# Reordering quarter products around a split S1 T1, in a relational graph layer on one core

## Chip, cores and metric

The kernel runs on one core of one Trainium2 chip. The metric is the device time of one execution in microseconds (us), as the median of several runs. Beside it there is one profiled execution, from which all durations of single instructions come.

## What is computed

A graph layer over N = 1250 nodes with D = 1024 features, R = 8 edge types and 20000 edges, all in fp32:

```python
h = maximum(layernorm(x), 0)
u = h @ root + bias
for r in range(8):                       # mean over the edges of type r into a node
    u = u + (segment_sum(h[src] * mask_r, dst) / maximum(cnt_r, 1)) @ weight[r]
z = concatenate([u, h]) @ w_gate + b_gate
out = x + tanh(u) * z + h * (1 - z)
```

## The kernel before

**Matrices and pairs.** The kernel multiplies first and sums over edges later. It forms h times each of the eight edge-type matrices (numbers 0 to 7), h times `root` (8) and h times the lower half of `w_gate` (9), stores these rows to HBM, and gathers them per edge. The last stage multiplies the finished u by the upper half of `w_gate` (10). The 1250 nodes are ten blocks of 128 rows, taken as five *pairs* (i = 0 to 4). So the outer loop is over matrices s = 0 to 9, the inner one over pairs, each a call of `step(s, i)`.

**One pair's product.** `product` (L388) multiplies two row blocks by a 1024x1024 matrix with seven products of half size instead of eight (the Winograd form of Strassen's method). Each has 128 rows, 512 of the inner dimension and 512 columns, and is four calls in `add` (L401), each of which is two TensorE instructions of 512 columns. Names: P1 = A11 B11, P2 = A12 B21, P3 = S4 B22, P4 = A22 T4, P5 = S1 T1, P6 = S2 T2, P7 = S3 T3. S are sums of blocks of h, T sums of blocks of the matrix (`make_t1` to `make_t4`, on VectorE). P1, P6, P7 and P4 build up in one PSUM bank `b`, and after each ScalarE copies the running sum out (L445, L468, L427, L493) before the next may be added. P5 goes to a bank `c`, is copied (L453), and P3 is added to it.

**Quarter products.** Pairs 0 and 1, and pairs 2 and 3, share work once more: the two P2 products of such a pair of pairs are done together by seven quarter products (class `Second`, object `e`). From matrix 4 on (`thirds(s)`) the same is done for P3 (class `Third`, `q`) and P1 (class `First`). A quarter product is `Second.add` at L218: four instructions of 256 columns. The fifth pair (i = 4) has no partner and is called the lone pair here; it does P2 and P3 itself.

**PSUM.** There are eight banks: a ring of four named `ps` (`bank()`), two named `ps_b` (`lead()`), and one each of `ps_q` and `ps_n`. A bank is written again only after its readers are done.

**Order of the work.** Every engine works through its own list in program order, and this order is written by hand. `done()` (L407) counts the steps of a product and calls `between(j)`. That hook puts other engines' work beside TensorE's: sums on VectorE, weight loads on the ScalarE and SyncE queues, and the edge work (a gather by GpSimd into one of four buffers at L1268, then multiply and add into a node's row on VectorE at L1273), spread evenly over the steps, seven to a product. `filled(name)` puts the quarter products behind the named product, by the dictionary `fill` in `step` (L623 to L657).

In pairs 0 and 2, P5 comes first, into `ps_n` (`hold`, L283). `First.late` (L350) then gives P1: six calls, and a copy at L353. In pair 0, `e.second` follows (with its add at L249), then P6, then P7 at once. In pairs 1 and 3, `then` (`Third.last` and `last_to`, L300 to L317) runs three quarter products between P6 and P7, and VectorE adds them at L313, L314 and L315. Pair 3 begins with `e.fourth`, which adds to a bank that ScalarE has just copied at L235; `q.first` (L290) comes behind it, and `e.second` between P7 and P4.

`First.early` (L339), the first four quarter products of a coming pair's P1, runs ahead of P4 in pairs 1 and 4. Behind it VectorE makes the sums of L278 to L281 for `First.late`. The sums of L272 to L275 serve `First.early`, and in pairs 0 and 2 `Third.first`.

**Row tiles.** Results collect in row tiles, of which there are four, each stored to HBM by SyncE (`put`, L551). The two tiles of pair 4 are those of pair 2. One of these is complete only in pair 3, and is stored there, after the add at L249.

Of the kernel before, what the change touches and what calls it, by code (L numbers as in the profile page):

```python
# [9 lines left out]
F32 = mybir.dt.float32  # L10
# [9 lines left out]
def tile_rgcn_highway(  # L20
# [35 lines left out]
    P = 128  # L56
# [4 lines left out]
    KQ = KC // 2  # L61
# [59 lines left out]
    def bank():  # L121
        return psum.tile([P, 512], F32, name="ps", bufs=4)
# [135 lines left out]
    class Third:  # L258
# [29 lines left out]
            Second.add(self, c[:, :H], self.a12, self.b21)  # L288

        def first(self):  # L290
            self.b = psum.tile([P, 512], F32, name="ps_q", bufs=1)[:, :H]
            self.c = bank()[:, :H]
            self.p = rows.tile([P, Q], F32, name="part", bufs=2)
            Second.add(self, self.b, self.a11, self.b11, True)
            nc.scalar.copy(self.p[:, :H], self.b)
            Second.add(self, self.c, self.s1, self.t1, True)
            Second.add(self, self.b, self.s2, self.t2)
            nc.scalar.copy(self.p[:, H:], self.b)
# [87 lines left out]
                                                                     aop[:, b])  # L386

    def product(aop, w, to, between=lambda j: None, last=None, pieces=1, whole=True,  # L388
                fill=None, second=None, third=None, inner=None, first=None, early=None):

        c11, c12 = to[0][:, :Q], to[0][:, Q:]
        c21, c22 = to[1][:, :Q], to[1][:, Q:]
        step = [0]

        def add(b, i, fresh=False, at=slice(0, Q)):  # L401
            for k in range(KQ):
                nc.tensor.matmul(b[:, at], aop[:, i, k, :], w.of[i][:, k, at],  # L403
                                 start=(fresh and k == 0), stop=(k == KQ - 1),
                                 skip_group_check=True)

        def done():  # L407
            between(step[0])
            step[0] += 1

        def filled(name):
            if fill and name in fill and fill[name]():
                done()

        def p3():
            add(c, S4)
            if third:
                third(c)
            else:
                nc.vector.tensor_add(c12, c12, c)  # L420
            done()
            filled("third")

        def p7():
            d = rows.tile([P, Q], F32, name="part", bufs=2)
            add(b, S3)
            nc.scalar.copy(d, b)  # L427
            nc.vector.tensor_add(c22, c22, d)  # L428
            done()
            filled("seventh")  # L430
            return d

        def p2():
            a = bank()
            add(a, A12, True)
            nc.vector.tensor_add(c11, c11, a)
            done()

        def p1():
            if first is None:  # L440
                b = lead()
                add(b, A11, True)
            else:
                b = first.late() if inner.holds else first.to1
            nc.scalar.copy(c11, b)  # L445
            done()
            filled("first")
            return b

        def p5():  # L450
            c = inner.hold() if inner and inner.holds else bank()
            add(c, S1, True)
            nc.scalar.copy(c22, c)  # L453
            done()
            filled("fifth")
            return c

        if first and inner.holds:
            c = p5()
            b = p1()  # L460
        else:
            b = p1()
            if second:
                second()
                p2()
            c = p5()
        add(b, S2)
        nc.scalar.copy(c12, b)  # L468
        done()
        filled("sixth")  # L470
        if whole and not third:
            p3()
            d = p7()
            if not second:
                p2()
        else:
            if inner and not inner.holds:
                inner.then(c)
                done()
                filled("third")  # L480
            d = p7()
            if third:
                last(d, 0)
            if not inner:
                p3()
        if early:
            early()
        if pieces == 1:
            add(b, A22)
            if last:  # L490
                last(b, 0)
            else:
                nc.scalar.copy(c21, b)  # L493
        else:
            for j in reversed(range(pieces)):
                at = slice(j * Q // pieces, (j + 1) * Q // pieces)
                b = bank()
                add(b, A22, True, at)
                last(b[:, at], at.start, d[:, at])
        done()  # L500
        filled("fourth")
# [27 lines left out]
    def step(s, i, between=lambda j: None, second=None):  # L529
# [80 lines left out]
        if two:  # L610
            e, to = waiting[i - i % 2]
            if thirds(s):
                if i % 2 == 0:
                    waiting_third[i] = Third(fac[s], i, room)
                q = waiting_third[i - i % 2]
                q.holds = i % 2 == 0

                def then(c):
                    q.last(c)
                    q.last_to(to[:, Q:], t[0][:, Q:], c)  # L620

                q.then = then
            if i == 0:  # L623
                fill = dict(sixth=lambda: (e.second(), e.second_to_first(to)))
                if q:
                    fill = dict(first=fill["sixth"], seventh=lambda: (q.second(q.c0), True))
            elif i == 1:
                fill = dict(first=lambda: (e.first(), q and q.first(), 0)[-1],
                            fifth=lambda: (e.sixth(), True),
                            sixth=lambda: (e.seventh(), e.to_first(to), 0)[-1])  # L630
                if q:
                    fill.update(third=lambda: (e.fourth(), e.to_second(t[0]),
                                               put(i - 1, 0, to), 0)[-1],
                                seventh=lambda: (e.fourth_to_second(t[0]), 0)[-1])
                else:
                    fill.update(seventh=lambda: (e.fourth(), e.to_second(t[0]),
                                                 put(i - 1, 0, to), 0)[-1],
                                third=lambda: (e.fourth_to_second(t[0]), 0)[-1])
            elif i == 2 and q:
                fill = dict(first=lambda: e.first(),  # L640
                            sixth=lambda: (q.second(q.c0), True),
                            seventh=lambda: e.sixth(),
                            fourth=lambda: (e.seventh(), e.to_first(to), True))
            elif i == 2:
                fill = dict(sixth=lambda: e.first(),
                            seventh=lambda: e.sixth(),
                            third=lambda: (e.seventh(), e.to_first(to), 0)[-1],
                            fourth=lambda: (e.fourth(), True))
            elif q:
                fill = dict(first=lambda: (e.fourth(), e.to_second(t[0]),  # L650
                                           e.fourth_to_second(t[0]), q.first(), 0)[-1],
                            seventh=lambda: (e.second(), True),
                            fourth=lambda: (e.second_to_first(to), put(i - 1, 0, to), 0)[-1])
            else:
                fill = dict(first=lambda: (e.to_second(t[0]), e.fourth_to_second(t[0]), 0)[-1],
                            sixth=lambda: (e.second(), True),
                            seventh=lambda: (e.second_to_first(to), put(i - 1, 0, to), 0)[-1])  # L657
        product(h_op[i], fac[s], t, between=beside, whole=not two, fill=fill, second=second,
                inner=q, first=waiting_first.get((s, i - i % 2)) if two else None,
                early=early if coming else None)  # L660
        for part in range(2):
            if part or not two or i % 2:
                put(i, part, t[part])
# [80 lines left out]
    with ExitStack() as early:  # L744
# [226 lines left out]
        def slots(ix):  # L971
# [78 lines left out]
            def place(j):  # L1050
                cs, o = chunks(j), now.pop(j)
                m, c0 = len(cs), cs[0]
                c1 = c0 + m
                p = psum.tile([P, 512], F32, name="ps_q", bufs=1)
                for i in range(m):
                    nc.tensor.matmul(p[:, i * 2 * NHI:(i + 1) * 2 * NHI], o["to_lo"][:, i, :],
                                     o["s_b"][:, i].rearrange("p a b -> p (a b)"),
# [184 lines left out]
    with ExitStack() as edges_part:  # L1242
# [358 lines left out]
        for i in range(NP):  # L1601
# [49 lines left out]
                    scatter_piece(c0, t[1])  # L1651

            if i < NP - 1:
                product(h_op[i % 2], fac[NM - 1], t, between=beside_u,
                        last=lambda *of: finish(1, *of))
                outs.append((2 * i + 1, t[1]))
            else:
                product(h_op[i % 2], fac[NM - 1], t, between=beside_last, last=finish_last,
                        pieces=2, second=lambda: None,
                        third=lambda c: finish(0, c, Q, rows.tile([P, Q], F32, name="part",  # L1660
                                                                  bufs=2)))
# [22 lines left out]
```

## Time and profile before

| what | value |
|---|---|
| median of 3 runs (lowest to highest) | 1363.49 us (1363.39 to 1367.92) |
| the profiled execution: time | 1361.2 us |
| the profiled execution: span, first to last instruction | 1359.4 us |
| VectorE, ScalarE, GpSimd busy | 73%, 28%, 44% of the span |
| granted TensorE clock, mean | 0.997 |
| bytes moved by DMA | 271.18 MB, 199 GB/s in the mean |
| one matrix of 4 to 9, start to start | 117 to 122 us |

The span is the profile's own measure; the execution's time is 1.8 us more. In the rows of a profile, PE is TensorE's matmuls, PEld its weight loads, DVE VectorE, ACT ScalarE, POOL GpSimd, SP SyncE. `L403` is line 403 of the kernel. `ps_b<-w,h_op` means that `ps_b` is written from `w` and `h_op`. `128x512` are partitions and elements of one instruction. Line 403 is every full product, line 218 every quarter product, and the bank's name tells which.

### The profile page before, as it was taken

Reading aid. Unit: us, or ns where it says so; the run is one execution under the profiler, and the core shown is the slowest. Engines: PE = TensorE matmul, PEld = TensorE weight load, DVE = VectorE, ACT = ScalarE, POOL = GpSimd, SP = SyncE. Lnnn points to the kernel's source line nnn. Section 1 sums busy time; section 2 is a strip of 40 time slices with the busy share of each in tenths; the row PEclk is TensorE's granted clock in tenths of the full one; section 3 lists DMA queues with packets and bytes.
Section 4 is the critical chain, followed back from the end, with each engine's and each line's share of the span. In section 5 each row is a group of like instructions: output and inputs, shape, how many; then the busy total and the mean of one; then the engine's idle time right before and its main releaser. Section 6 shows DMA issues by size and latency. Waiting matters only on the chain. (4 is left out here: it accounts for less than half of the span.)

```text
span 1359.4 us, 13672 instructions
## 1 busy us (share of the span) xinstructions
PE 1336.1 (98%) x4098; PEld 712.2 (52%) x4098; DVE 995.2 (73%) x2049; ACT 384.1 (28%) x852; POOL 592.6 (44%) x510
## 2 busy tenths in 40 slices
PE   9999999999999999999999999999999999999997
PEld 5444455455445545655664555565465456644443
DVE  7855967876785835526877887987778789777875
ACT  3335566465741112211121211122122111221210
POOL 0001655654652466001454554555455546534731
PEclk9999999999999999999999999999999999999999
DMA  9744675754764251144647778788778958889961
GB/s 317 271 177 150 103 131 143 210 84 110 175 166 111 54 153 34 47 155 151 206 132 293 241 237 320 281 262 307 245 248 294 337 180 239 265 286 286 350 169 58
DMA packets 106911, 271.18 MB, mean 199 GB/s; under 512 B 22692, under 2 KB 24946, under 8 KB 106704
## 3 DMA queue, kind: packets, MB, share of 16 engines
q1 hardware_dynamic: 46640, 120.01, 29.2%
q0 software_dynamic: 44064, 118.28, 27.5%
q10 hardware_dynamic: 16128, 31.98, 7.4%
q8 instruction: 32, 0.52, 0.2%
q14 instruction: 47, 0.39, 0.1%
HBM read 212.71 MB, written 75.66 MB: 212 GB/s over the span
## 5 line engine op out<-in xcount | busy, mean ns | idle before, releaser
L403 PE MATMUL ps_b<-w,h_op 128*128 128x512 f32 x1560 | 702.1, 595 | 5.0 <-ACT row L468 4.1
L403 PEld LDWEIGHTS ps_b<-w,h_op 128*128 128x128 f32 x1560 | 291.6, 190 | 334.5 <-issue 316.9
L1268 POOL DMA_INDIRECT got<-y,idx x193 | 261.6, 1355 | 335.8 <-DVE u L1273 206.0
L403 PE MATMUL ps<-w,h_op 128*128 128x512 f32 (+1 forms) x760 | 340.3, 591 | 3.0 <-ACT row L453 3.0
L1273 DVE SCALAR_TENSOR_TENSOR u<-got,w_of,u 128x1024 f32<-128x1024 f32 (+1 forms) x193 | 246.9, 1282 | 54.1 <-DMA got<-y,idx 47.3
L1084 POOL DMA_INDIRECT table<-row_col,at_i x157 | 175.5, 1118 | 160.0 <-DVE at_i L1080 76.9
L403 PEld LDWEIGHTS ps<-w,h_op 128*128 128x128 f32 x760 | 143.8, 191 | 167.7 <-issue 161.2
L427 ACT COPY part<-ps_b 128x512 f32<-128x512 f32 x55 | 32.2, 585 | 218.2 <-PE ps_b L403 218.2
L428 DVE TENSOR_TENSOR row<-row,part 128x512 f32<-128x512 f32 x54 | 37.2, 689 | 70.2 <-ACT part L427 70.2
L493 ACT COPY row<-ps_b 128x512 f32<-128x512 f32 x49 | 28.6, 584 | 185.8 <-PE ps_b L403 185.8
L468 ACT COPY row<-ps_b 128x512 f32<-128x512 f32 x54 | 31.6, 585 | 146.0 <-PE ps_b L403 145.9
L218 PE MATMUL ps<-w,h_op 128*128 128x256 f32 x264 | 69.0, 384 | 2.8 <-ACT w L235 2.8
L218 PE MATMUL ps<-w,w 128*128 128x256 f32 x288 | 71.3, 380 | 0.0
L218 PEld LDWEIGHTS ps<-w,w 128*128 128x128 f32 x288 | 54.4, 190 | 20.9 <-issue 14.8
L218 PEld LDWEIGHTS ps<-w,h_op 128*128 128x128 f32 x264 | 49.1, 190 | 26.6 <-issue 16.1
L453 ACT COPY row<-ps 128x512 f32<-128x512 f32 x42 | 24.6, 585 | 120.1 <-PE ps L403 104.4
L1070 DVE SCALAR_TENSOR_TENSOR junk<-k_bc,key_col,before 128x128 f32<-128x128 int32 x157 | 55.0, 350 | 4.2
L1010 DVE TENSOR_TENSOR seen<-seen,ps_n 128x100 f32<-128x100 f32 x157 | 40.2, 256 | 24.3 <-PE ps_n L1005 20.1
L445 ACT COPY row<-ps_b 128x512 f32<-128x512 f32 x54 | 31.7, 587 | 89.8 <-PE ps_b L403 83.7
L173 DVE TENSOR_TENSOR w<-w,w 128x2048 f32<-128x2048 f32 (+1 forms) x12 | 25.4, 2115 | 41.4 <-PE ps L403 41.2
L218 PE MATMUL ps<-inner,inner 128*128 128x256 f32 x192 | 49.4, 380 | 1.2 <-DVE inner L273 1.2
L420 DVE TENSOR_TENSOR row<-row,ps 128x512 f32<-128x512 f32 x29 | 19.8, 684 | 41.9 <-PE ps L403 30.7
(236 smaller groups left out, 1460.2 us busy)
## 6 DMA issues: line engine op xcount, KB each, us to landing
y<-row SPq DMA_DIRECT2D x72, 512.0 KB
w<-in_L_gnn_weight_dram ACTq DMA_DIRECT2D x21, 1024.0 KB
w<-in_L_gnn_weight_dram SPq DMA_DIRECT2D x10, 1024.0 KB
k_bc<-keys_dram SPq DMA_DIRECT2D x39, 256.0 KB
l_bc<-los_dram SPq DMA_DIRECT2D x39, 256.0 KB
w<-in_L_gnn_w_gate_dram ACTq DMA_DIRECT2D x6, 1024.0 KB
h_dram<-h_op SPq DMA_DIRECT2D x9, 512.0 KB
u<-in_L_gnn_bias_dram SPq DMA_DIRECT2D x9, 512.0 KB
```

The costliest lines, as they stand in the source:

```text
L218: nc.tensor.matmul(p, a[:, k, :], b[:, k, :], start=(fresh and k == 0), stop=(k == 1), skip_group_check=True)
L403: nc.tensor.matmul(b[:, at], aop[:, i, k, :], w.of[i][:, k, at], start=(fresh and k == 0), stop=(k == KQ - 1), skip_group_check=True)
L427: nc.scalar.copy(d, b)
L428: nc.vector.tensor_add(c22, c22, d)
L445: nc.scalar.copy(c11, b)
L468: nc.scalar.copy(c12, b)
L493: nc.scalar.copy(c21, b)
L1010: nc.vector.tensor_add(seen[j][:, i, :], was, p[:, i, :])
L1070: nc.vector.scalar_tensor_tensor(junk, o["k_bc"][:, i, :], key_col[:, c:c + 1], before, op0=OP.is_equal, op1=OP.mult, accum_out=rank[:, c: ...
L1084: ins = nc.gpsimd.indirect_dma_start(out=table[:, :], out_offset=bass.IndirectOffsetOnAxis(ap=at_i[:n, i:i + 1], axis=0), in_=row_col[:n, ...
L1268: nc.gpsimd.indirect_dma_start(out=t[:n], out_offset=None, in_=y[g][:, :], in_offset=bass.IndirectOffsetOnAxis(ap=at[:n, d, k:k + 1], axis=0),
L1273: nc.vector.scalar_tensor_tensor(u[:n], t[:n], w, u[:n], op0=OP.mult, op1=OP.add)
```

## The change

- **First pair (i = 0, matrices 4 to 9).** P5 is cut in two: half of its inner dimension ahead of `First.late`, half behind it. `e.second` moves from behind P1 to behind P6.
- **Fourth pair (i = 3).** `q.first` comes ahead of `e.fourth`. `e.second` moves from between P7 and P4 to between P6 and P7, and its add at L249 behind P7. `then` moves from between P6 and P7 to between P7 and P4. The store of the row tile moves from behind P4 to behind `then`. The second pair keeps its order, since it has an `early`.
- **Lone pairs (from matrix 4) and the last stage.** P5 takes the bank `ps_n` and P2 the bank `ps_q`, instead of two of the ring of four.
- Three allocations of `ps_q` get the same shape; that is a matter of form.

```diff
-        def add(b, i, fresh=False, at=slice(0, Q)):
-            for k in range(KQ):
+        def add(b, i, fresh=False, at=slice(0, Q), ks=range(KQ)):
+            for k in ks:
...
+        def held(name):
+            if not own:
+                return bank()
+            return psum.tile([P, CG, P], F32, name=name, bufs=1).rearrange("p c k -> p (c k)")
+
         def p2():
-            a = bank()
+            a = held("ps_q")
...
-        def p5():
-            c = inner.hold() if inner and inner.holds else bank()
-            add(c, S1, True)
+        def p5(c=None):
+            if c is None:
+                c = inner.hold() if inner and inner.holds else held("ps_n")
+                add(c, S1, True)
+            else:
+                add(c, S1, ks=range(KQ // 2, KQ))
...
-        if first and inner.holds:
+        if first and inner.holds and early is None and "first" not in fill:
+            c = inner.hold()
+            add(c, S1, True, ks=range(KQ // 2))
+            b = p1()
+            p5(c)
+        elif first and inner.holds:
             c = p5()
             b = p1()
...
-            if inner and not inner.holds:
+            def then():
                 inner.then(c)
                 done()
                 filled("third")
+
+            if early:
+                then()
             d = p7()
             if third:
                 last(d, 0)
             if not inner:
                 p3()
+            elif not early and not inner.holds:
+                then()
...
                 fill = dict(sixth=lambda: (e.second(), e.second_to_first(to)))
                 if q:
-                    fill = dict(first=fill["sixth"], seventh=lambda: (q.second(q.c0), True))
+                    fill["seventh"] = lambda: (q.second(q.c0), True)
...
             elif q:
-                fill = dict(first=lambda: (e.fourth(), e.to_second(t[0]),
-                                           e.fourth_to_second(t[0]), q.first(), 0)[-1],
-                            seventh=lambda: (e.second(), True),
-                            fourth=lambda: (e.second_to_first(to), put(i - 1, 0, to), 0)[-1])
+                fill = dict(first=lambda: (q.first(), e.fourth(), e.to_second(t[0]),
+                                           e.fourth_to_second(t[0]), 0)[-1],
+                            sixth=lambda: (e.second(), True),
+                            seventh=lambda: (e.second_to_first(to), 0)[-1],
+                            third=lambda: (put(i - 1, 0, to), 0)[-1])
...
-                early=early if coming else None)
+                early=early if coming else None, own=s > EARLY and not two)
...
-                product(h_op[i % 2], fac[NM - 1], t, between=beside_u,
+                product(h_op[i % 2], fac[NM - 1], t, between=beside_u, own=True,
...
-                product(h_op[i % 2], fac[NM - 1], t, between=beside_last, last=finish_last,
+                product(h_op[i % 2], fac[NM - 1], t, between=beside_last, last=finish_last, own=True,
```

More of the change, by code (lines that the diff above doesn't have):

```diff
@@ L290, in first @@
         def first(self):
-            self.b = psum.tile([P, 512], F32, name="ps_q", bufs=1)[:, :H]
+            self.b = psum.tile([P, CG, P], F32, name="ps_q", bufs=1).rearrange(
+                "p c k -> p (c k)")[:, :H]
             self.c = bank()[:, :H]
@@ L388, in product @@
     def product(aop, w, to, between=lambda j: None, last=None, pieces=1, whole=True,
-                fill=None, second=None, third=None, inner=None, first=None, early=None):
+                fill=None, second=None, third=None, inner=None, first=None, early=None, own=False):
         c11, c12 = to[0][:, :Q], to[0][:, Q:]
@@ L1053, in place @@
                 c1 = c0 + m
-                p = psum.tile([P, 512], F32, name="ps_q", bufs=1)
+                p = psum.tile([P, CG, P], F32, name="ps_q", bufs=1).rearrange("p c k -> p (c k)")
                 for i in range(m):
```

## Prediction, made before the changed kernel was run

> **What bounds the kernel now.** I read the page's engine shares first, then TensorE's own waits, then the timelines around each wait.
>
> ```profile
> PE 1336.1 (98%) x4098; PEld 712.2 (52%) x4098; DVE 995.2 (73%) x2049; ACT 384.1 (28%) x852; POOL 592.6 (44%) x510
> ```
>
> TensorE is the bound: of the 1359.4 us span only 23.3 are not busy, 1.4 at its start and 7.8 at its end among them. The change neither adds nor removes a matmul, so it can only touch what TensorE waits for:
>
> ```profile
> PE ps_b L403 <- ACT row L468: 4.1, 6, 0.7
> PE ps L403 <- ACT row L453: 3.0, 1, 3.0
> PE ps L218 <- ACT w L235: 2.8, 6, 0.5
> PE ps L369 <- DVE row L420: 1.5, 1, 1.5
> ...
> PE ps L218 <- DVE inner L273: 1.2, 1, 1.2
> ```
>
> Columns: who waits, for what, total us, times, longest. The first row is the first pair (S2 T2, then S3 T3), the third the fourth pair (a quarter product after the copy at L235), each once in each of matrices 4 to 9. The second and fourth happened once, and lie with the lone pair and the last stage. These idle times are understated, because a matmul's end is modelled; I cost with starts. Weight loads show the pitch of a 512-column instruction: 0.19 us and 0.24 idle, 0.43. A product (eight) takes 3.44, a quarter product (four of 256 columns) 0.86 (515.67 to 516.54 for one of them).
>
> First pair, timeline of TensorE and ScalarE (start, us, engine, line, what, and in brackets the idle time before it and what ended it):
>
> ```profile
> 519.25 3.60 PE L403 MATMUL ps_b<-w,h_op 128*128 128x512 f32 x8
> ...
> 522.88 0.58 ACT L468 COPY row<-ps_b 128x512 f32<-128x512 f32 x1 [4.69 <-PE ps_b L403]
> 523.52 3.70 PE L403 MATMUL ps_b<-w,h_op 128*128 128x512 f32 x8 [0.68 <-ACT row L468]
> ```
>
> S2 T2 could be followed at 519.25+3.44 = 522.69. The next product writes the bank being copied, so it starts at 523.52: 0.83 lost. The group that waited is also 0.10 longer (3.70 against 3.60).
>
> Fourth pair:
>
> ```profile
> 579.82 1.03 PE L218 MATMUL ps<-w,w 128*128 128x256 f32 x4
> 581.30 1.13 PE L218 MATMUL ps<-w,h_op 128*128 128x256 f32 x4 [0.46 <-ACT w L235]
> ```
>
> The second could start at 579.82+0.86 = 580.68: 0.62 lost, and 0.10.
>
> The one long stall, in the lone pair of the root matrix:
>
> ```profile
> 1077.12 0.34 DVE row L249
> ...
> 1077.47 8.81 DMA hr_dram<-row
> ...
> 1086.38 0.59 ACT row L453
> ...
> 1087.02 5.40 PE ps L403 x8
> ```
>
> This is the chain of waits. The store of the third pair's row tile waits for VectorE's add at L249. It takes 8.81 us to land; only then may the copy at L453 overwrite the tile, and only then may TensorE add S4 B22 to the bank that is copied. The instruction before it began at 1083.42, so it could have gone on at 1083.85: 3.17 lost.
>
> **The change, part by part.** Sums are against the profiled execution (span 1359.4, time 1361.2); the median of the runs is 1363.49, 2.3 above it, and I subtract from the median.
>
> *First pair.* Half of S1 T1 (four instructions) now stands behind the First quarter products and covers the copy at L445; `e.second`, which did that, moves behind S2 T2 and covers the copy at L468. Cover 0.86 against 0.83 lost: just enough. The same spacing is already in the trace, later in the same pair: one quarter product (`q.second`) covers the copy of S3 T3's bank, and A22 T4 writes that bank next:
>
> ```profile
> 527.05 1.03 PE L218 MATMUL ps_n<-w,h_op 128*128 128x256 f32 x4
> 527.92 1.10 PE L403 MATMUL ps_b<-w,h_op 128*128 128x512 f32 x2
> ```
>
> No idle time, but 1.10 for two instructions where 1.02 is normal: a wait met just in time costs 0.08. Gain 0.83+0.10-0.08 = 0.85, six times: 5.1 us. At worst the 0.08 is 0.10. The copy at L445 keeps more cover (four instructions, 1.72 us, instead of 0.86).
>
> What the move exposes: the First quarter products start 1.72 us earlier and need VectorE's sums of L278 and L279. L279 ended before they began by 5.2, 5.2, 2.6, 3.6, 2.7 and 2.2 us in the six matrices, so by 0.5 to 3.5 after the move. The sums follow, on VectorE, an add on TensorE's own result (ScalarE's L427, then L428), so they shift with TensorE. Bounds: 0 (no wait), and 4 us (VectorE 2 us later in the four tight matrices: 1.1+0.1+1.0+1.5, and their 0.10s). I take 0.3, by the rows' slacks. VectorE's hooks all move with their step; its `e.second_to_first` (L249) stands one hook later, and who waits for it is the fifth-product bank of the next pair, over 8 us away.
>
> *Fourth pair.* `q.first` (three quarter products, 2.59 us) goes ahead of `e.fourth`, and covers the copy at L235: gain 0.72, six times, 4.3 us. Inside it, ScalarE has L235, L445 (0.59) and L295 in its queue; L295 ends about 1.45 us after the quarter product starts, its reader comes at 1.72: free. `e.second` (0.86) now covers L468 where the inner products (2.59) did: +0.08; these cover L427 in its stead: -0.08. VectorE's L256 waits 2 us longer for `e.fourth`, and behind it stand `next_sums`; their reader comes 3.7 us later than before. ScalarE's weight load (L140) and SP's wait on L253 stay at their steps; the make_t1 that reads these loads is over 15 us away.
>
> *The store.* It now waits for L249 and L313, and both stand ahead of the fifth hook's gather-adds on VectorE instead of behind two hooks of them. With L428 near 1069 and one gather-add behind it, the store leaves near 1072 and lands near 1081 at 8.8 us; the copy is wanted done by 1083.8, so must start by 1083.2. On SP's queue the store passes only what the sixth hook issues (a store of finished rows, L1481); that stood ahead of it and now waits behind it, but for less long than the store waited before, and its data is read a stage later. What the stall cost:
>
> ```profile
> 1084.00:1087.00 3.00, 0.01 (x1) 0.00 (x0) 1.98 (x5) 0.62 (x2) 1.53 (x1) 1.00 1.03 417
> 1087.00:1088.50 1.50, 1.48 (x4) 0.68 (x5) 0.76 (x1) 0.45 (x1) 0.00 (x0) 0.94 1.03 419
> 1088.50:1092.00 3.50, 3.50 (x6) 1.51 (x5) 0.52 (x1) 0.00 (x0) 0.99 (x1) 0.54 1.03 415
> ```
>
> Third number from the end: granted clock, 0.54 after the stall. The eight instructions took 1087.02 to 1092.25, 5.23 instead of 3.44. The Trainium skill ("TensorE: Matmul & The Clock Gate", "What's actually happening") has the clock fall to half only after an idle window of about 3.4 us. By that rule a stall of 3.0 is free of it and this part is worth 3.2; by the row it is worth 3.17+1.79 = 4.96. The row decides. Bounds 0 (the DMA share is full at 1.03, the store may land no sooner) and 5.0; I take 5.0, by the 2 us of margin.
>
> *Lone pairs and last stage.* Fifth and second product leave the ring of four `ps` banks. The transpose that waited for L420 (twelve transposes from 1261.19 end by 1262.50, the next began at 1264.17) then has a bank of the pair before: 1.7 us. The price would be that `ps_n` is one bank deep: the lone pair's fifth product waits for L313. The skill ("PSUM — Partial Sum Buffer", "Summary: rules for kernel authors") says to evacuate promptly; this change reads `ps_n` later. By the rule, no cover, each of six would cost a VectorE add, about 0.9 us and 5 in all; by the rows, in the fourth pair L313 ended 0.9 us behind its product (2.4 once), and the taker comes 7.7 us behind it. I take 0.
>
> *The L273 wait* (second pair; 1.24 and 0.16 and 0.10 by starts, 1.5). Not touched, but TensorE gets there 0.85 earlier, while VectorE was late by a gather. Bounds: 1.5 gained, 2.2 lost over it and the next tight one (0.4 us slack in matrix 9). I take 0.4 lost.
>
> Sum: 5.1+4.3+5.0+1.7-0.3-0.4 = 15.4. Profiled time 1345.8; median **1348.0 us**.
>
> **Rivals.**
> 1. *VectorE becomes what ends the waits.* 4.0 at the First sums and 2.2 at L273: 15.4 falls to 9.9, 1353.6. For it: VectorE is 77 to 83% busy in matrices 5 to 9 (DVE busy over the length of such stretches), slacks of 0.5. Against: tied to TensorE's own results. Chance 0.15.
> 2. *The store lands no sooner* (full DMA): 5.0 stays, 1353.0. With rival 1 as well, 1358.6. Chance 0.13.
> 3. *More than seen*: the runs' median is 2.3 above the profiled one; if that is longer store stalls, they go too: 1345.7, and 1343.6 with the L273 wait gone. Chance 0.12.
> 4. *Slower*: the one-deep `ps_n`. If L313 ended more than 7.7 us behind its product, each lone pair would stall; a stall of 3 cools the clock, 4.9 each, six times 29: 1377. It outweighs the gains from 2.6 us per lone pair, L313 10.3 us behind. The worst L313 in the trace is 5 us behind, in the second pair. Chance 0.02.
> 5. *The moves do nothing* (the waits reappear one product on): 1363. The just-in-time row speaks against it. Chance 0.03.
>
> The forecast has 0.55. **Range** 1342 to 1356: below, rival 3 with 1.6 to spare; above, rivals 1 and 2 singly with some 2.5 to spare; both together, 4 and 5 lie outside. A measurement here tells about 0.5%, 6.8 us, from no change. Faster by more 0.91, within 0.06, slower 0.03.
>
> **What would show it.** TensorE's waits lose the L468 rows of the first pair, L235, L453 and L420; the L403 group after S2 T2 shows the 0.08; granted clock stays at 1.00 through the root matrix; PE busy stays near 1334 (without the cold 1.8). Wrong if a new wait on L279, L313 or L273 stands in the table with over 3 us, or if L453 is still released by a DMA with TensorE behind it.

## The result, and the profile after

The changed kernel takes 1354.6 us (median of 7 runs, 1352.04 to 1357.04) against 1362.28 (7 runs, 1361.54 to 1367.92) for the kernel before on the same chip: ratio 0.9935 [0.9918, 0.9952]. The interval leaves out 1, so the kernel is faster, but the gain is 7.7 us by the medians (8.9 by the ratio) where 15.4 was forecast. The two profiled executions are 1355.7 and 1361.2 us long, with spans of 1353.9 and 1359.4: 5.5 us between them. Below, matrices are numbered 4 to 9, and 8 is `root`. Lines after L281 have moved; those of the text:

| what | before | after |
|---|---|---|
| full product (TensorE) | L403 | L404 |
| copy of P6 (ScalarE) | L468 | L483 |
| copy of P5 in a lone pair (ScalarE) | L453 | L463 |
| P3's add in `then` (VectorE) | L313 | L314 |
| gather-add of the edge work (VectorE) | L1273 | L1294 |

The engine shares on the page. TensorE is busy for as long as before (1336.1), where the forecast had 1334: the cold stretch behind the store's stall went, and another came:

```profile
PE 1336.0 (99%) x4098; PEld 714.9 (53%) x4098; DVE 993.8 (73%) x2049; ACT 384.4 (28%) x852; POOL 596.0 (44%) x510
```

TensorE's waits (who, for what, total us, times, longest):

```profile
PE ps L218 <- DVE inner L279: 4.7, 1, 4.7
PE ps L218 <- DVE inner L273: 1.9, 1, 1.9
...
PE ps_b L404 <- ACT row L483: 0.8, 1, 0.8
```

Every row that the change was to remove is gone: the first pair's copy, L235, the store behind L453, the transposes behind L420. In their place stands one wait of 4.7 us for a VectorE sum that had no row before, and the wait for L273 is longer. A wait of over 3 us for L279 is one of the prediction's own signs of being wrong. The last row is a wait in the last stage (at 1335), not one of the six first pairs; before, the profile had it under "issue" (0.7).

First pair, timelines of TensorE and ScalarE in matrix 4:

```profile
522.03 1.03 PE L218 MATMUL ps<-w,h_op 128*128 128x256 f32 x4
522.89 3.67 PE L404 MATMUL ps_b<-w,h_op 128*128 128x512 f32 x8
```

```profile
522.23 0.58 ACT L483 COPY row<-ps_b 128x512 f32<-128x512 f32 x1 [2.85 <-PE ps_b L404]
```

The quarter product starts as S2 T2 ends, ScalarE copies the bank meanwhile, and S3 T3 follows 0.86 later with no idle time. S3 T3 takes 3.67 where 3.60 is normal: about the 0.08 of a wait met just in time. In the fourth pair the quarter products follow each other 0.86 apart, with no idle time for L235:

```profile
579.16 1.03 PE L218 MATMUL ps<-w,w 128*128 128x256 f32 x4
580.02 1.03 PE L218 MATMUL ps_q<-w,h_op 128*128 128x256 f32 x4
```

The store left at 1071.98 instead of 1077.47 (SyncE's queue). The copy behind it still waited for the store to land; TensorE did not, but only just:

```profile
1077.94 0.59 ACT L463 COPY row<-ps_n 128x512 f32<-128x512 f32 x1 [5.39 <-DMA hr_dram<-row]
```

```profile
1078.97 3.60 PE L404 MATMUL ps_n<-w,h_op 128*128 128x512 f32 x8
```

The second line is S4 B22, which needs the copy: it was done 0.44 before. The new wait lies 30 us further on, at the first pair of matrix 9. TensorE there:

```profile
1096.16 1.88 PE L404 MATMUL ps_n<-w,h_op 128*128 128x512 f32 x4
1102.73 2.08 PE L218 MATMUL ps<-inner,inner 128*128 128x256 f32 x4 [4.69 <-DVE inner L279]
1104.60 1.91 PE L218 MATMUL ps_b<-w,inner 128*128 128x256 f32 x4
```

The 1.88 is half of S1 T1, four instructions of 0.43, so `First.late` could have started at 1097.88. It started 4.85 later, and then took twice its usual time: the pitch between quarter products is 1.87 and 1.70 instead of 0.86. The windows show the granted clock (third number from the end):

```profile
1103.50:1108.50 5.00, 5.00 (x13) 3.87 (x12) 4.97 (x6) 1.16 (x2) 4.37 (x2) 0.51 0.34 115
...
1080.00:1095.00 15.00, 15.00 (x44) 8.13 (x44) 10.45 (x12) 1.31 (x3) 5.60 (x4) 1.00 1.02 390
```

From this pair's First products to the second pair's is 50.35 instead of the untroubled 47.59, so the cold clock costs another 2.76, 7.61 in all: the 4.96 of the store's stall before, and half as much again. The second row, just before the wait, has the DMA engines full (1.02, the number after the clock).

**Where the forecast went**, by starts, from First products to First products: each untroubled matrix of 4 to 9 is 1.6 us shorter (117.38 became 115.78), some 9.4 for six. The stall of 4.96 and the transposes' 1.7 are gone, so 16.1 was won. Lost were 7.61 at L279, 2.36 more at L273 (3.86 with its cold clock of 1.68, against 1.5) and 0.39 at the `ps_n` bank of the root matrix's lone pair. That leaves 5.7, and the span fell by 5.5. The root matrix itself went from 122.35 to 121.17, where the end of its stall (5.0) and the 1.6 should have given 6.6.

**What VectorE did there.** Its own waits between 985 and 1105 us, before and then after:

```profile
DVE u L1273 <- DMA got<-y,idx: 14.0, 12, 2.5
DVE u L1273 <- issue: 4.1, 1, 4.1
DVE row L420 <- PE ps L403: 3.5, 1, 3.5
DVE row L428 <- ACT part L427: 2.6, 2, 2.2
```

```profile
DVE u L1294 <- DMA got<-y,idx: 22.0, 16, 3.8
DVE row L249 <- ACT row L483: 2.2, 1, 2.2
DVE u L1294 <- issue: 1.4, 1, 1.4
```

With 1.7 us of small rows before, the sums are 25.9 and 25.6. VectorE waits as long as it did; what it had waited for TensorE and ScalarE's copies it now waits for gathers. So its pace hardly changed: from the end of L279 in matrix 8 to that in matrix 9 it needs 122.8 us before and 121.9 after, while TensorE's step without its wait would be 121.17 - 4.85 = 116.3. The 5.6 between them, less the 0.8 by which L279 was early in matrix 8, is the wait of 4.8.

The chain of waits through that stretch shows the same (start, us, what):

```profile
1074.74 10.18 DMA got<-y,idx
...
1086.57 8.21 DMA got<-y,idx
...
1097.92 2.29 DVE w L181
```

The gather of 1074.74 was issued in a burst of stores and a weight load and took 10.2 us to land. VectorE had waited 3.80 for it:

```profile
1085.01 1.28 DVE L1294 SCALAR_TENSOR_TENSOR u<-got,w_of,u 128x1024 f32<-128x1024 f32 x1 [3.80 <-DMA got<-y,idx]
```

From 1085.01 to 1102.67 VectorE is at work with only 0.76 us idle: what the hooks put there (gather-adds, `make_t2` and `make_t3` at L177 and L181), adds on TensorE's results, and the sums for matrix 9 last.

### The profile page after: what moved, and what is told of

Read it like the earlier page. It is cut to its first block, busy times and chain, and to the rows that moved or that the text cites. A ratio compares the mean times of both kernels' runs of the same rounds, so it can differ in the third digit from the quotient of the medians.

```text
span 1353.9 us, 13649 instructions
## 1 busy us (share of the span) xinstructions
PE 1336.0 (99%) x4098; PEld 714.9 (53%) x4098; DVE 993.8 (73%) x2049; ACT 384.4 (28%) x852; POOL 596.0 (44%) x510
## 4 chain that ended last, share of the span: by engine, by line
PE 74%; DMA 11%; issue 7%; DVE 4%; POOL 3%; ACT 0%; POOLq 0%; SPq 0%; DVEq 0%; ACTq 0%
PE ps_b L404 38%; PE ps L404 15%; PE ps L218 10%; DMA got<-y,idx 8%; PE ps_n L404 4%; PE ps_b L218 2%; PE ps_q L218 2%; DVE u L1294 1%; PE ps_n L218 1%; DMA h_op<-z_dram,node 1%; POOL got L1289 1%; DMA got<-hr_dram,node 1%; PE ps_q L404 1%; PE ps L370 1%; POOL got L709 1%
## 5 line engine op out<-in xcount | busy, mean ns | idle before, releaser
L404 PE MATMUL ps_b<-w,h_op 128*128 128x512 f32 x1560 | 702.4, 595 | 1.0 <-ACT row L483 0.8
L404 PEld LDWEIGHTS ps_b<-w,h_op 128*128 128x128 f32 x1560 | 291.9, 190 | 329.6 <-issue 319.0
L1294 DVE SCALAR_TENSOR_TENSOR u<-got,w_of,u 128x1024 f32<-128x1024 f32 (+1 forms) x193 | 246.9, 1282 | 58.8 <-DMA got<-y,idx 55.1
L404 PE MATMUL ps<-w,h_op 128*128 128x512 f32 (+1 forms) x496 | 220.1, 587 | 0.0
L404 PEld LDWEIGHTS ps<-w,h_op 128*128 128x128 f32 x496 | 93.2, 190 | 100.7 <-issue 98.3
L404 PE MATMUL ps_n<-w,h_op 128*128 128x512 f32 x272 | 123.6, 593 | 0.1
L404 PEld LDWEIGHTS ps_n<-w,h_op 128*128 128x128 f32 x272 | 51.9, 191 | 63.1 <-issue 60.8
L483 ACT COPY row<-ps_b 128x512 f32<-128x512 f32 x54 | 31.6, 585 | 136.5 <-PE ps_b L404 136.4
L218 PEld LDWEIGHTS ps<-w,h_op 128*128 128x128 f32 x264 | 49.6, 190 | 24.3 <-issue 18.5
```

The lines of the kernel that those rows point to most:

```text
L218: nc.tensor.matmul(p, a[:, k, :], b[:, k, :], start=(fresh and k == 0), stop=(k == 1), skip_group_check=True)
L1294: nc.vector.scalar_tensor_tensor(u[:n], t[:n], w, u[:n], op0=OP.mult, op1=OP.add)
```

## Experiments

Two theories. *VectorE's order*: the sums at L278 and L279 stand behind the hooks' work, VectorE with its gathers is as slow as TensorE through matrices 8 and 9, and what is won on TensorE there comes back. *The split*: half of S1 T1 moved behind `First.late` takes 1.72 us of cover from the sums, so without the split there would be no wait. A third, *the gathers*: the burst of transfers alone makes VectorE late. (The texts for e1 to e6 call the first and third together the gather theory; from x0 on the first is called the VectorE theory.) Ratios are against the kernel before on the same chip, whose median was between 1362.3 and 1370.1 on the chips of this study.

| run | median us | ratio | idle for L279 / L273, us |
|---|---|---|---|
| e1_first_pair | 1365.84 | 0.9981 [0.9960, 1.0002] | 0 / 5.2 |
| e2_fourth_pair | 1362.57 | 0.9961 [0.9941, 0.9980] | 2.8 / 2.8 |
| e3_banks | 1366.68 | 0.9985 [0.9966, 1.0003] | 0 / 1.3 |
| e4_no_split | 1358.31 | 0.9925 [0.9897, 0.9954] | 2.0 / 3.6 |
| e5_no_loads | 1350.68 | 0.9904 [0.9888, 0.9919] | 3.1 / 2.8 |
| e6_sums_first | 1361.71 | 0.9983 [0.9965, 1.0001] | 1.1 / 7.9 |
| e7_both_sums | 1355.45 | 0.9935 [0.9920, 0.9951] | 1.0 / 4.6 |
| x0_changed_again | 1357.05 | 0.9916 [0.9883, 0.9949] | 4.2 / 2.0 |
| x1_no_t2_t3 | 1352.03 | 0.9878 [0.9848, 0.9908] | 0 / 3.0 |
| x4_late_store | 1356.52 | 0.9905 [0.9872, 0.9938] | 5.8 / 2.0 |
| x6_early_sums | 1354.40 | 0.9898 [0.9867, 0.9928] | 4.6 / 0 |
| y2_t3_behind | 1353.19 | 0.9916 [0.9899, 0.9934] | 0 / 2.3 |

Runs on one chip: e1 to e4; e5 to e7; x0 to x6. The kernel before had 1369.21, 1363.55 and 1370.12 there, and 1365.01 beside y2.

**One part alone (e1, e2, e3).** e1 is the kernel before with the split, and `e.second` behind P6:

```diff
-                    fill = dict(first=fill["sixth"], seventh=lambda: (q.second(q.c0), True))
+                    fill["seventh"] = lambda: (q.second(q.c0), True)
```

> The kernel before with the first pair's part alone (S1 T1 in two halves, e.second behind P6). Gather theory (in the root matrix's lone pair VectorE waits for gathers on a full DMA, and whatever TensorE wins there it waits for at the sums of L278 and L279): the store's stall of 3.2 us stays and still gives the gathers their time, so the 5.1 us of the first pairs are kept whole and the L279 wait is under 0.5 us; about 1357 against 1362. Split theory (the wait comes from the First quarter products starting 1.7 us earlier): L279 shows 3 us or more here too, and the gain is 2 us or less.

The 0.7s of the first pair are gone; L235 stays (2.8), the store's stall too. Its profiled execution was the longest of its 12 runs (1378.95), so its rows are not a middle case: the root matrix took 129.2, and the stall was 5.6:

```profile
PE ps L403 <- ACT row L456: 5.6, 1, 5.6
```

With the split but with the stall still there, no wait for L279; but with a stall this long that says little about one of 3.0. The gain is 2.6 us by the ratio, with 5.5 at the end of its interval: below the 5.1 of that part, but not shown to be less, nor shown to be more than nothing.

e2 is the kernel before with the fourth pair's order (`then` behind P7 and the new `fill` for i = 3):

> The kernel before with the fourth pair's part alone (q.first first, e.second, then and the store moved). Gather theory: the store's stall (5.0 with the slow clock) goes, but TensorE then waits about 3 us for L279 in matrix 9 (4.7 less the 1.7 of the whole S1 T1), 3 to 5 us with the clock; net gain 4 to 6, about 1357. Split theory: no wait at L279, gain 4.3+5.0 = 9, about 1353.

```profile
PE ps L218 <- DVE inner L273: 2.8, 2, 1.6
PE ps L218 <- DVE inner L279: 2.8, 1, 2.8
```

The stall and L235 are gone, the first pair's row is there as before (4.5 in seven places), and the wait for L279 is there *without the split*. So the split is not needed for it; it came with the fourth pair's part, in which the stall goes. e3 is the kernel before with `held` and `own`:

> The kernel before with the banks alone (lone pairs and last stage take ps_n and ps_q). Both theories: the transposes' wait of 1.7 us in the last stage goes, the store's stall stays; gain 1 to 2 us, hardly more than the noise. The one-deep ps_n shows no wait, since the inner products are read early in this order.

The transposes' wait is gone, the others stay (store 3.9, L235 2.8), and in the lone pairs TensorE never waits for the `ps_n` bank to come free (the store's 3.9 is in a row of `ps_n`, since P3 adds there). By the ratios the three gains, 2.6, 5.3 and 2.1, make 10, between what the whole change gave on the first chip (8.9) and on that of x0 (11.5). Within these wide intervals no interplay of the parts shows in the medians.

**The change without the split (e4).** The first pair has its old order, `e.second` behind P1 included; the `fill` line goes back as well:

```diff
-        if first and inner.holds and early is None and "first" not in fill:
-            c = inner.hold()
...
-        elif first and inner.holds:
+        if first and inner.holds:
             c = p5()
             b = p1()
```

> The changed kernel with the first pair in its old order, the rest changed. Gather theory: L279 wait in matrix 9 of about 3 us (4.7 less 1.7), and the six L468 waits of the first pair come back (5.1): about 1357 to 1358. Split theory: no wait at L279, so 7 us less of stall and 5.1 more of L468: about 1352.

The wait for L279 is 2.0 and not 4.7, shorter by 2.7, of which the split's moving TensorE ahead is 1.7; the first pair's waits are back (L478 here, 4.8 in seven places, 0.8 of it in the last stage), and the granted clock stays at 1.00 behind the wait. The theory of the split falls as a cause; the split is a term in the size. And with a ratio of 0.9925 against 0.9935 and 0.9916 for the whole change (on two other chips), no gain of the split is left to see: the forecast 5.1 stands against 2.7 of idle time and 2.76 of cold clock.

**Fewer transfers (e5).** Leaves out two weight loads of matrix 9, 1 MB each, in the root matrix's lone pair, so matrix 9 is computed from wrong weights:

```diff
-                    new.load_b22()
+                    if s != NM - 3:
+                        new.load_b22()
```

> The changed kernel without the two 1 MB weight loads that the root matrix's lone pair issues for matrix 9 (its b22 and b21 keep old contents, so matrix 9's output is not the reference's). Gather theory: without these 2 MB the gathers land sooner, VectorE's waits for got there fall from about 10 us to under 5, the L279 wait of 4.7 us falls under 1.5, and the time is 5 to 8 us below the changed kernel's. Rival (VectorE's own order of work is late, whatever the DMA does): L279 stays at 4 to 5 us, the time within 2 us of the changed kernel's.

The wait only falls to 3.1, between the two forecasts, and the clock stays up. The late gather lands earlier, but VectorE then works from 1081.64 to 1098.43 without a stop, 16.8 us, much as before. The theory of the gathers falls as the whole cause.

**Less work for VectorE (x1).** The opposite half: leaves out `make_t2` and `make_t3` of matrix 9 (again wrong values), two instructions of 2.28 us, and nothing else:

```diff
-                elif j == 4:
+                elif j == 4 and s != ROOT:
...
-                elif j == 5:
+                elif j == 5 and s != ROOT:
```

> The changed kernel without make_t2 and make_t3 for matrix 9 (two subtractions of 2.28 us on VectorE in the root matrix's lone pair; matrix 9's output is not the reference's). VectorE theory: 4.6 us less work in the stretch that sets L279, the wait falls from 4.7 to under 0.5 and the clock stays up: 5 to 8 us below the changed kernel. Rival (the gathers' landing alone sets it): the freed time turns into waits for got on VectorE, L279 moves by under 2 us, and so does the time.

```profile
PE ps L218 <- DVE inner L273: 3.0, 3, 1.3
```

The wait for L279 is gone, and VectorE's step from L279 to L279 is 118.9 instead of 121.6 in x0: 2.7 of the 4.6 taken out. The rest of the wait went because TensorE lost about 2.3 at other waits of the root matrix (by starts, at L273 and for the copy L463), and L279 was met just in time (its group takes 1.13). The median is 5.0 below that of x0, the unaltered changed kernel on the same chip, with runs that do not overlap:

> The changed kernel unaltered, beside the next three on one chip, so that they have a common base. About 0.9935 of the kernel before (1354 to 1356). TensorE's wait for L279 in matrix 9 stands again, 3 to 5 us: the theory (in the root matrix VectorE with its gathers is the bound, and never waits for TensorE) has it there in every run; if it were one execution's accident it would be missing.

x0 shows the same two waits (4.2 and 2.0), and a step of 121.6 from L279 to L279. So less VectorE work and fewer transfers each shorten the wait, and neither is shown to be its whole cause: the sums end a row of VectorE work that begins with a late gather.

**Moving the sums (e6, e7, x6).** e6 puts the lone pair's `early` with its sums ahead of the hook that holds `make_t3` and the gather-adds:

```diff
             nc.vector.tensor_add(c11, c11, a)
+            if early and whole:
+                early()
             done()
...
-        if early:
+        if early and not whole:
             early()
```

> The changed kernel with First.early and its sums ahead of the fifth hook in lone pairs, so ahead of make_t3 (2.3 us) and a gather-add (1.3) on VectorE. Gather theory: the sums come 3.5 us sooner whatever the gathers do; the L279 wait falls from 4.7 to 1 to 1.5 us and the clock stays up, 6 us less: about 1348.5. The L273 wait stays. Rival (a gather just ahead of the sums sets the time): the wait stays over 3 us.

```profile
PE ps L218 <- DVE inner L273: 7.9, 3, 4.3
```

The wait for L279 at the First products is gone (1.1 is left at other places), and a larger one stands at L273, with 4.3 in one place of matrix 9; TensorE also waits 0.8 for L314 and 1.5 for a copy of ScalarE's in the root matrix's lone pair, both ahead of the moved sums. The time is 1361.7, where 1348.5 was expected. VectorE has as much to do as before, and something is last. x6 instead brings forward the sums of L272 to L275 in the second pair, into `then`:

```diff
-            if coming and j == (4 if i == 1 else 2):
+            if coming and i != 1 and j == 2:
                 first_sums()
...
+                    if coming and i == 1:
+                        first_sums()
```

> The changed kernel with the sums of L272 to L275 ahead of the three adds of last_to in second pairs (2.1 us of VectorE). The L273 wait in matrix 6 (1.9, with the slow clock 3.9) falls under 0.3, L279 in matrix 9 is untouched: 2 to 4 us below the changed kernel. If VectorE is the bound there as well, the wait comes back further on in matrix 6 or 7 and the gain is under 1.

```profile
PE ps L218 <- DVE inner L279: 4.6, 1, 4.6
```

The wait for L273 in matrix 6 is gone for good, and that matrix takes 115.97 instead of 119.83. L279 stays, as it should. The median is 2.65 below x0's on that chip; the intervals overlap, so it may be better than the changed kernel, but is not shown to be. e7 is e6 with x6's edit:

> As the run before, and in second pairs the sums of L272 to L275 ahead of the three adds of last_to (2.1 us of VectorE). The L273 wait of 1.9 us in matrix 6 (3.9 with the slow clock) falls under 0.3; the sums of the inner products' results come 2.2 us later, and nobody near waits for them. About 1345, 3 to 4 us below the run before.

Its ratio is that of the changed kernel (measured on another chip), and short of the 1345 expected. Only the move of x6 lies between e6 and e7, and the profiles show that it acts in more than one second pair: the waits for L273 in matrices 6 (2.0) and 7 (1.6) are gone, and those matrices take 2.8 and 1.8 less; the one in matrix 9 falls from 4.3 to 2.5, and the time from its First products on by 4.1; but the root matrix, with a new wait of 2.1 for L273, takes 3.1 more. The spans differ by 5.0.

**Moving `make_t3` (y2).** x6, with `make_t3` for matrix 9 one hook later, behind the sums:

```diff
-                elif j == 5:
+                elif j == (6 if s == ROOT else 5):
```

> The kernel with the early sums of second pairs, and make_t3 for matrix 9 one hook later, behind the sums of L278 and L279 instead of ahead of them (one subtraction of 2.28 us on VectorE, no work left out). If the L279 wait is VectorE's order just there, it falls from 4.6 to about 2.3 us, the clock stays up, and the 6.9 us of stall and slow clock become 2.4: 3 to 4.5 us below the kernel with the early sums, 0.986 to 0.987 of the kernel before. If VectorE is the bound through matrices 8 and 9 alike, the 2.3 us come back as another wait for VectorE in matrix 9 and the gain is under 1 us.

```profile
PE ps L218 <- DVE inner L273: 2.3, 1, 2.3
PE ps_n L404 <- ACT row L463: 1.9, 1, 1.9
PE ps_n L404 <- DVE row L314: 0.9, 1, 0.9
```

L279 is gone, and three others stand in the table; the root matrix took 119.68 (x6 120.6), and the rest from there 250.9 (x6 249.8), so the profile shows no gain. But the two `ps_n` waits lie at 1071 and 1080, ahead of the moved instruction, so the move did not make them, and they gave VectorE some 3 us at the sums. So y2 fits VectorE as the bound of the whole stretch, and does not show it.

**The store's place (x4).** The changed kernel with the store put back behind P4:

```diff
-                            third=lambda: (put(i - 1, 0, to), 0)[-1])
+                            fourth=lambda: (put(i - 1, 0, to), 0)[-1])
```

> The changed kernel with the store of the third pair's row tile back behind P4, all else changed. VectorE theory: L463's copy waits for the store again (TensorE 2 to 4 us in the root matrix's lone pair), and the L279 wait shrinks by as much; the root matrix stays at 120 to 122 us and the time within 2 us of the changed kernel. Rival (bringing the store forward is a gain of its own, the L279 wait a cost of its own): 3 to 5 us slower, with both waits.

TensorE still does not wait for the store, and the time is that of x0; both expectations had such a wait. So the store's place in SyncE's list does nothing. By elimination it is that L249 and L314 come ahead of the hooks' gather-adds on VectorE; no run changes that alone.

The stall is also not gone for good. From the store's leaving to the start of the copy behind it are 5.2 to 6.0 us in the changed kernel, x0, x4, x6, e5 and e2, but 7.5 in x1 and 8.6 in e7, where TensorE waits 0.9 and 2.1 for the copy (in e6 and y2, 1.5 and 1.9, with the copy's own wait put down to a weight load). Why the time differs the runs do not show.

## Why the prediction was right and wrong

- *First and fourth pair, 0.85 and 0.72 a matrix.* Right where TensorE is the bound: 1.6 a matrix together, and the 0.08 is in the row. The measured gain of e1 alone was smaller than its part, and its interval is wide.
- *The store, 5.0.* The stall and its cold clock are gone (right), and the store left at 1072 as worked out. But the margin of 2 us was luck in part: the deadline of 1083.8 was read in the old trace, and in the changed kernel TensorE reached S4 B22 at 1078.97, 4.9 earlier. It did not wait because the copy could start 5.96 after the store left, not 8.81; with 8.81 it would have lost some 2.5 us (an estimate from these times). By x4, the store's own place counts for nothing.
- *Transposes, 1.7, and the lone pairs at 0.* Right but for 0.39 once: in the root matrix's lone pair L314 ended 8.0 us behind its product (1063.99 to 1071.95), past the 7.7 that the fourth rival's text gave as the limit, and TensorE lost 0.29 and 0.10. The slower case was near, and stayed at a single place.
- *L273, 0.4 lost.* The bound was 2.2; it was 2.36, because the idle of 1.9 us was followed by a cold clock (1.68).
- **The step that failed**: "so they shift with TensorE", with 0.3 taken for the First sums. It was 7.61, beyond the bound of 4. In five of the six matrices the sums did end 0.8 to 3.5 ahead, as forecast (0.5 to 3.5); in matrix 9 they were 4.8 late. The step took the sums' slack from a trace in which the root matrix still had its stall of 5 us. VectorE depends on TensorE's results, but in that matrix it hardly waited for them (some 7.8 us of 25.9 for TensorE and ScalarE). When these come earlier it waits for the gathers instead (14.0 became 22.0). The stall had been VectorE's slack. The bound of 4 added up what a VectorE 2 us late would cost in four matrices, and left out both the 5 us that the store's part takes from the same slack, and the cold clock after a wait.
- *Rivals.* The first (VectorE ends the waits) came true, though with its loss at the First sums in one matrix and not in four; its 1353.6 is nearer to the 1354.6 measured than the forecast's 1348.0. The second (the store lands no sooner) did not happen here, by 0.44 us. The third can't be told: on the chip where the kernel before was slower (1370.1), the change was worth 11.5 us by the ratio (0.9916 [0.9883, 0.9949]), with an interval that overlaps that of the first chip; what its runs lose there no profile shows.

Open: what makes the store land in 5 us or in 8, the chip's part in the gain, and how the wait at L279 divides between the gathers and VectorE's own work. A deeper ring of gather buffers, which would let gathers run ahead of the burst, was not tried.

## What to carry to other kernels

Before counting a gain on the bound engine, look at the next engine's waits in the same stretch: if it waits little for the bound engine, and for something else most of the time, it may not come earlier with it. A slack read from a trace with a stall in it is slack only as long as the stall stands; subtract the gain from every slack behind it, over all parts of the change together. And price a new wait with the clock that follows it, here between nothing and 0.9 of the idle time again.

## What the runs showed of the hardware

In these runs no length of idle time separates the waits after which the granted clock fell from those after which it stayed. After 1.9 us of idle (matrix 6 of the changed kernel) it fell to half for a while; after 2.8 us (e2, the wait for L279) it stayed, as it did after 3.1 in e5, and after 2.0 at the same place of matrix 6 in x0:

```profile
788.00:790.50 2.50, 2.50 (x7) 2.00 (x6) 2.36 (x5) 0.00 (x0) 1.91 (x1) 0.50 0.60 243
```

```profile
1107.28:1111.28 4.00, 4.00 (x17) 3.25 (x18) 4.00 (x4) 1.16 (x2) 3.40 (x2) 1.00 0.58 170
```

Nor is its length fixed: after some 4.7 us of idle it was still 0.51 from 1103.5 to 1108.5 in the changed kernel, and in x6 it was back at 1.00 from 1102.5, 2.9 us after TensorE went on. Gathers of 512 KB issued into the burst of the root matrix took 8.2 and 10.2 us to land with the DMA share at 1.02. VectorE waited for such gathers for 22.0 us of that stretch, so its busy share (73% of the whole) did not show that its pace was TensorE's.
